# Five two-level products, added in DRAM, in the second stage of the two middle blocks

## The chip, the cores and the metric

The kernel runs on one core of one Trainium2 chip. The metric is the device time of an execution in microseconds; the figure for a kernel is the median of its runs. All arithmetic is fp32.

## What is computed

```python
def _L0_cond_ref(v, q, W3, b3, W2, b2):            # v: (64, 64, 512), q: (64, 256)
    q_emb = jax.nn.relu(q @ W3 + b3)
    n = v.shape[1]
    v_sum = jnp.sum(v, axis=1, keepdims=True)
    x = (n * v + v_sum) * q_emb[:, None, :]
    return jax.nn.relu(x @ W2 + b2)                # W2: (512, 512)

def _L0_ffn_ref(x, W_base, b_base, A_s, B_s, A_r, B_r, W_router, b_router):
    base_out = x @ W_base + b_base                 # W_base: (512, 512)
    shared_out = (x @ A_s) @ B_s                   # rank 16
    gates = softmax(x @ W_router + b_router)       # 6 experts, the best 2 count
    ...
    h = jnp.einsum('bsd,edr->bser', x, A_r)        # rank 16 each
    routed_out = jnp.einsum('bser,erf->bsf', h * w_per_e[..., None], B_r)
    return base_out + shared_out + routed_out

return x + _L0_ffn_ref(_L0_cond_ref(x, cond, ...), ...)
```

There are 4096 tokens of width 512, in 64 batches of 64. Each token goes through two products with a 512 x 512 matrix, a ReLU between them, and a low-rank term.

## The kernel before

**Blocks and stages.** The tokens are cut into NB = 4 blocks of 1024 (k = 0 to 3), each into two halves of TB = 512 columns; features lie on the partitions, in four chunks of 128. A block passes a first stage (`y = relu(x @ W2 + b2)`, in `first_mixed` for k = 0 and `first_inner` for the others) and a second stage (`out = x + y @ W_base + ...`, in `second`, and in `second_inner` for k = 3). Between them stand the low-rank matmuls with `a_sb` (`ph`, L1225), whose results `gate`, `weigh` and `turn` make into `hwT`, the weighted and transposed low-rank rows; `difference` makes `hwd`, the difference of its two halves.

**Seven products instead of eight.** Both 512 x 512 products are done by the Strassen-Winograd scheme: the operands are 2 x 2 in blocks of 256 features by 512 tokens, and seven products of block sums are combined. For the second stage the sums of `y` are made by `row_sums` (tile `sy`) and the sums of the weights are `tb`. With p1 to p7 the products, y = p1 + p6 and z = y + p7, the four output quarters are p1 + p2, y + p5 + p3, z + p4 and z + p5 (each with its share of the low-rank term and of x). The carried sums y and z are built by seeding: ScalarE copies one PSUM bank into another, and TensorE adds to it there. A plain product is done by `product`: for each of two output chunks, two matmuls of 512 columns (L181).

**Two levels.** A product can be done by the same scheme once more: seven matmuls of 128 x 128 x 256 (q(1) to q(7) in the code) instead of four of 512 columns. `inner_tools` has its steps. For product number t of its order, `open_banks(t)` takes two PSUM banks, `seed_y` and `seed_z` are ScalarE copies inside PSUM, and `take_w5`, `take_u`, `take_22`, `take_11`, `take_12` and `take_21` bring quarters out. A take without a summand (`plus` is None) is a ScalarE copy, except `take_22` and `take_12`, which add on VectorE to what lies in the destination. q(3) overwrites what `take_w5` reads, and q(4) what `take_22` reads. The sums of the moving operand (four operations of 128 x 256 each) are made by `inner_row_steps`, mostly on GpSimd. `row_places` says where they lie.

**Where which is used.** In the first stages of k = 1 to 3 all seven products are on two levels (matmuls at L488). In the second stage k = 0 has none, k = 3 has five (1, 2, 5, 4, 3), and k = 1 and 2 have two: products 1 and 2, in `two_products`, whose parts are handed to `second` through `two`. There products 3, 4, 5, 6 and 7 are plain. The routed term is a matmul of `bcat_sb` with `hwT` or `hwd` into the same banks (L778, 512 columns each), and the results are added to the rows of `x` (`res`, loaded by `load_rows`) by VectorE (`with_x`, `finish`, `leave`), from where SP's queue stores them.

**Order.** The order of instructions on each engine is written out by hand: an engine works through its list in the order of the calls, and waits at semaphores for the others. The next block's preparation is spread among the steps: `prepare(k + 1)` puts ScalarE's modulation of `x` (L224, 128 x 64 each, in pairs) on a list `behind`, from which `fill(n)` takes n pairs, and VectorE's sums for the next first stage on a list `held`, from which `sums_ahead(n)` takes n steps. GpSimd's part of the next first stage (`inner_two`, `s`, `inner_s`, `inner_late` at L334 to L337 and L278, then the sums at L585 and L588) comes in its list after all that the second stage gives it.

**Buffers.** `x` has three buffers (`xpool`), one of which becomes `wide`: the weight sums of products 5, 4 and 3, and the `parts` of two products. The tags `u`, `u22`, `u21` and `u12` hold the first stage's parts and then the rows of `x`. PSUM has six banks for products and two for `ph`, `pt`.

Of the kernel before, what the change touches and what calls it, by code (L numbers as in the profile page):

```python
# [10 lines left out]
F32 = mybir.dt.float32  # L11
# [27 lines left out]
def adaln_ffn(ctx: ExitStack, tc: tile.TileContext, xa, x0, x1, head, w3, w2, wb, a, bcat, bb, br, outT):  # L39
# [164 lines left out]
    def modulate(k):  # L204


        vs[k] = v = xs[k]
# [14 lines left out]
        def batch(c, b):  # L222
            x = v[:, c, :, ts(b, NH)]
            nc.scalar.activation(x, x, AF.Identity, bias=vsum[:, c, b : b + 1], scale=nq[:, c, b : b + 1])  # L224
# [71 lines left out]
    def prepare(k, also=()):  # L296
# [28 lines left out]
        behind.extend(pairs)  # L325
        if k == 1:
            behind.extend([step] for step in late + prepare_inner(k))
        else:

            held.extend(sums[c2] + sums[c3] + early + late[:3] + prepare_inner(k, late[3]))  # L330
# [9 lines left out]
    def prepare_inner(k, fourth=None):  # L340
# [37 lines left out]
        return first + steps("sums", of_s(all_of), nc.vector, all_of)  # L378
# [87 lines left out]
    def first_inner(k, y):  # L466
# [77 lines left out]
        open_banks(1)  # L544
        for t in range(2):
            q(1, t)
            q(5, t)
            seed_y(t)
            take_w5(t)
# [133 lines left out]
    def load_rows(k):  # L683

        res = {}
        for n, (f, h) in zip(pair_tags[2:3] + pair_tags[:2] + pair_tags[3:], ((1, 0), (1, 1), (0, 0), (0, 1))):
            res[f, h] = tmp.tile([P, KH, TB], F32, tag=n, name=f"x{n}_{k}")
            nc.sync.dma_start(
                res[f, h], x1[k, f * KH : (f + 1) * KH, :, ts(h, TB)].rearrange("c p t -> p c t")
            )  # L690
        return res

    def two_products(k, y, res):

        plain = mid.tile([P, 4, 4, R2], F32, tag="inner_s", name=f"inner_y_{k}")
        p1, p2 = wide["parts"][:, 0], wide["parts"][:, 1]
        operand = {1: y[:, :KH, 0], 2: y[:, KH:, 0]}
        s_side, sums_of = row_places(plain, lambda o: operand[o], {o: (o - 1, (0, 1, 2, 3)) for o in (1, 2)})
        tools = inner_tools(k, "h", (1, 2), low_side, s_side, {1: None, 2: None}, {1: p1, 2: p2})
        for o in (1, 2):  # L700
            for step in sums_of(o, lambda c, r, o=o: operand[o][:, c, ts(r, R2)], nc.gpsimd):
                step()

        def first_part():
            tools.open_banks(0)
            tools.q(1, 0)
            tools.q(5, 0)
            tools.seed_y(0)
            tools.take_w5(0)

        def second_part():
            tools.q(6, 0)
            tools.seed_z(0)
            tools.take_u(0)

        def third_part(ph):

            tools.open_banks(1)
            tools.q(1, 1)
            tools.q(5, 1)  # L720
            tools.seed_y(1)

            def first():
                tools.q(7, 0)
                tools.q(3, 0)
                tools.q(6, 1)
                tools.seed_z(1)
                tools.q(2, 0)
# [5 lines left out]
            tools.q(4, 0)  # L734
            tools.take_21(0)
            tools.q(7, 1)
            tools.take_22(1)
            tools.q(3, 1)
            tools.q(2, 1)

        def fourth_part(seeds):

            tools.take_u(1)
            tools.take_1(1)
            seeds[0]()
            tools.q(4, 1)
            seeds[1]()
            tools.take_21(1)
            tools.add(res[0, 0], res[0, 0], p2, nc.gpsimd)

        return {6: first_part, 7: second_part, "gate": third_part, "end": fourth_part, "p1": p1}

    def second(k, y, ph, res, two=None):
# [38 lines left out]
        ahead = [3, 0, 5, 1, 1, 2]  # L792

        def share():
            if two:
                sums_ahead(ahead.pop(0) if ahead else 0)
                return
# [5 lines left out]
        if two:  # L803
            copy_in = lambda name, j, source: nc.scalar.copy(bank(name, j), source)
            two["gate"](ph)
            weigh(k, ph)
            for j in range(KH):
                copy_in("y", j, two["p1"][:, j])
                prod(6, j, "y", start=False)
            fill(2)  # L810
            two["end"]([lambda j=j: seed("z", "y", j) for j in range(KH)])
            sums_ahead(2)
            for j in range(KH):
                u12[j] = with_x("y", j, KH + j, 0)
            for j in range(KH):
                copy_in("x", j, two["p1"][:, j])
            fill(2)
            prod(7, 0, "z", start=False)
            u22[0] = with_x("z", 0, KH, 1)
            sums_ahead(3)  # L820
            hwT = turn(k)
            prod(7, 1, "z", start=False)
            u22[1] = with_x("z", 1, KH + 1, 1)
            sums_ahead(1)
            fill(len(behind))
        else:
            gate(k, ph)
            prod(1, 0, "x")
            seed("y", "x", 0)
            prod(1, 1, "x")  # L830
            seed("y", "x", 1)
            prod(6, 0, "y", start=False)
            seed("z", "y", 0)
            prod(2, 0, "x", start=False)
            weigh(k, ph)
            u12[0] = with_x("y", 0, KH, 0)
            share()
# [451 lines left out]
```

## Time and profile before

| | |
|---|---|
| time, median of 3 runs | 257.36 us (257.3 to 257.56) |
| the profiled execution, its own time | 257.64 us |
| its span | 255.8 us |
| granted TensorE clock, mean | 0.998 |
| TensorE busy | 250.9 us in 1058 records |
| VectorE busy | 197.4 us in 389 |
| ScalarE busy | 152.2 us in 419 |
| GpSimd busy | 94.9 us in 116 |
| second stage, k = 1 (with the low-rank matmuls) | 94.6 to 133.4 us |
| first stage, k = 2 | 133.4 to 155.3 us |
| second stage, k = 2 | 155.3 to 194.1 us |
| stores, 256 KB each | 29, landing after 2.1 us |
| loads of rows of x, 512 KB each | 16, landing after 3.7 us |

The profile is of one execution; its span is the time from its first to its last instruction, and the execution's own time is longer by what lies around it. A fp32 matmul is two records in the trace. Records of TensorE are pipelined: the time from one start to the next is what a matmul costs, and it is shorter than the duration of a record. Line numbers (L488) are those of the kernel before. DMA transfers issued by SP are done by hardware queues; the trace of this kernel has no transfer issued by GpSimd.

### The profile page before, as it was taken

The page shows a single profiled execution, that of the slowest core. Times are in us where ns is not written, and L with a number is a line of the kernel's source. Part 1 is how long each engine was busy: PE and PEld are TensorE (multiplying, and loading weights), DVE is VectorE, ACT ScalarE, POOL GpSimd, SP SyncE. Part 2 cuts the span into 40 slices and gives each one's busy share as a digit, 9 for nine tenths or more (in the row PEclk, how much of TensorE's full clock was granted, in tenths as well). Part 3 has the DMA queues.
Part 4 walks back from the last instruction along what each step waited for, and adds up shares of the span by engine and source line. Part 5 has one row for each costly group of instructions (what it writes and reads, how often), then busy time and mean ns, then how long its engine had stood idle before and what let it go on. Part 6 is the DMA issues. An engine that isn't in the chain of part 4 may idle for free.

```text
span 255.8 us, 3426 instructions
## 1 busy us (share of the span) xinstructions
PE 250.9 (98%) x1058; PEld 175.8 (69%) x1058; DVE 197.4 (77%) x389; ACT 152.2 (59%) x419; POOL 94.9 (37%) x116
## 2 busy tenths in 40 slices
PE   8999999999999999999999999999999999999994
PEld 3755896454468889754458889955446889975783
DVE  2899998889967887895696797999296576887472
ACT  2299587688038799689306889689803427443220
POOL 1000000008008556037004988107200997039950
PEclk9999999999999999999999999999999999999999
DMA  6997729502420045000152023300044004400054
GB/s 179 383 342 271 309 67 379 210 3 83 163 82 0 3 129 195 6 3 0 46 201 83 0 86 110 138 3 0 0 164 164 0 0 157 175 3 1 0 184 143
DMA packets 14677, 28.55 MB, mean 112 GB/s; under 512 B 1490, under 2 KB 3538, under 8 KB 14659
## 3 DMA queue, kind: packets, MB, share of 16 engines
q1 hardware_dynamic: 14370, 28.08, 31.0%
q10 hardware_dynamic: 288, 0.26, 0.3%
q8 instruction: 8, 0.13, 0.2%
q14 instruction: 11, 0.08, 0.1%
HBM read 19.94 MB, written 8.39 MB: 111 GB/s over the span
## 4 chain that ended last, share of the span: by engine, by line
PE 94%; ACT 2%; DMA 2%; SPq 0%; issue 0%; DVE 0%
PE ia L488 13%; PE ph L1225 11%; PE ib L488 10%; PE oz L181 9%; PE ow L181 8%; PE py L395 5%; PE oy L181 5%; PE ja L894 4%; PE ow L778 4%; PE jb L894 4%; PE ha L894 3%; PE ox L181 3%; PE hb L894 2%; PE oz L778 2%; PE ox L778 2%; DMA w_sb<-in_w_dram 2%
## 5 line engine op out<-in xcount | busy, mean ns | idle before, releaser
L224 ACT ACTIVATE x<-x,vsum,nq 128x64 f32<-128x64 f32 x192 | 67.6, 433 | 1.3 <-DVE vsum L220 1.3
L1225 PEld LDWEIGHTS ph<-a_sb,y 128*128 128x128 f32 x256 | 30.9, 192 | 1.6 <-ACT y L381 0.7
L1225 PE MATMUL ph<-a_sb,y 128*128 128x118 f32 x256 | 31.4, 276 | 0.3 <-ACT y L381 0.3
L494 ACT COPY ib<-ia 128x256 f32<-128x256 f32 x21 | 7.5, 359 | 39.5 <-PE ia L488 39.5
L479 DVE TENSOR_TENSOR u<-ib,u 128x256 f32<-128x256 f32 x42 | 16.4, 417 | 14.0 <-PE ib L488 14.0
L639 POOL TENSOR_TENSOR hwd<-hwT 113x512 f32<-113x512 f32 x4 | 5.5, 1363 | 57.2 <-ACT hwT L634 57.2
L334 POOL TENSOR_TENSOR inner_two<-x 128x256 f32<-128x256 f32 x3 | 2.2, 725 | 48.7 <-PE ib L488 48.7
L479 DVE TENSOR_TENSOR u<-ia,u 128x256 f32<-128x256 f32 (+1 forms) x36 | 16.1, 461 | 5.0 <-ACT u L526 2.9
L381 ACT ACTIVATE y<-u,head_sb 128x256 f32<-128x256 f32 (+1 forms) x30 | 15.8, 584 | 3.6 <-DVE u L454 3.0
L488 PE MATMUL ib<-inner_s,inner_t 128*128 128x256 f32 x60 | 17.8, 384 | 0.0
L218 DVE TENSOR_REDUCE vsum<-x 128x8 f32<-128x512 f32 x24 | 15.4, 674 | 0.0
L181 PE MATMUL oz<-sy,tb 128*128 128x512 f32 x32 | 15.0, 593 | 0.0
L395 PE MATMUL py<-v,w_sb 128*128 128x512 f32 (+1 forms) x40 | 14.4, 510 | 0.3 <-DMA w_sb<-in_w_dram 0.3
L181 PE MATMUL oy<-sy,tb 128*128 128x512 f32 x32 | 14.6, 594 | 0.0
L887 POOL TENSOR_TENSOR xu<-xu,inner_tb 128x1024 f32<-128x1024 f32 x2 | 4.7, 2362 | 24.0 <-ACT inner_tb L910 24.0
L497 ACT COPY ib<-ib 128x256 f32<-128x256 f32 x21 | 7.6, 363 | 9.0 <-PE ib L488 8.9
L488 PEld LDWEIGHTS ib<-inner_s,inner_t 128*128 128x128 f32 x60 | 11.2, 190 | 2.2 <-ACT ib L497 0.8
L262 ACT ACTIVATE v<-x,vsum,nq 128x64 f32<-128x64 f32 x32 | 11.0, 428 | 1.9 <-DVE vsum L260 1.9
L275 DVE TENSOR_TENSOR s<-x 128x512 f32<-128x512 f32 x6 | 4.9, 824 | 9.3 <-ACT x L224 9.2
L395 PEld LDWEIGHTS py<-v,w_sb 128*128 128x128 f32 x40 | 7.4, 190 | 6.3 <-issue 4.5
L181 PE MATMUL oz<-y,tb 128*128 128x512 f32 x24 | 11.3, 592 | 0.0
L181 PE MATMUL ow<-sy,tb 128*128 128x512 f32 x24 | 11.3, 592 | 0.0
(270 smaller groups left out, 609.2 us busy)
## 6 DMA issues: line engine op xcount, KB each, us to landing
xu<-in_x_dram SPq DMA_DIRECT2D x16, 512.0 KB, 3.7
out_dram<-xu SPq DMA_DIRECT2D x29, 256.0 KB, 2.1
x<-in_x_dram SPq DMA_DIRECT2D x12, 512.0 KB, 7.6
x<-in_x_dram SPq DMA_DIRECT2D x7, 256.0 KB, 5.6
w_sb<-in_w_dram SPq DMA_DIRECT2D x4, 256.0 KB, 5.6
wb_sb<-in_wb_dram SPq DMA_DIRECT2D x4, 256.0 KB, 5.3
out_dram<-xu SPq DMA_DIRECT2D x4, 128.0 KB, 1.7
w_sb<-in_w_dram SPq DMA_DIRECT2D x1, 384.0 KB, 5.2
```

The lines of the kernel that those rows point to most:

```text
L181: nc.tensor.matmul(ps, w[i][:, c, ts(j, P)], s[i][:, c, :], start=start and c == 0, stop=c == KH - 1, skip_group_check=True,)
L218: nc.vector.tensor_reduce(vsum[:, c, bs], xc, AX.XY, ALU.add)
L224: nc.scalar.activation(x, x, AF.Identity, bias=vsum[:, c, b : b + 1], scale=nq[:, c, b : b + 1])
L262: nc.scalar.activation(v[:, c, :, ts(b, NH)], batches_of(c, b, b + 1)[:, :, 0], AF.Identity, bias=vsum[:, c, b : b + 1], scale=nq[:, c, b ...
L381: nc.scalar.activation(y[:, f, h, cols], src, AF.Relu, bias=b2_sb[:, f : f + 1])
L395: nc.tensor.matmul(p[:, :, lo * NH : hi * NH], w2_sb[:, c, ts(f, P)], v[:, c, :, lo * NH : hi * NH], start=(c == 0 and lo == 0), stop=(c = ...
L479: add = lambda o, a, b: nc.vector.tensor_tensor(o, a, b, ALU.add)
L488: nc.tensor.matmul(bank[b, t][:, cols], t_side(o, n), s_side(o, n), start=n == 1, stop=True, skip_group_check=True,)
L497: nc.scalar.copy(bank["b", t][:, hi], bank["b", t][:, lo])
L778: nc.tensor.matmul(ps[name, j], bcat_sb[:, ts(f, P)], hw, start=False, stop=True, skip_group_check=True)
L894: nc.tensor.matmul(p, w, s, start=start, stop=True, skip_group_check=True)
L1225: nc.tensor.matmul(ph[:, h * NS + s, :HC], y[:, c, h, ts(s, P)], a_sb[:, c, :], start=(c == 0), stop=(c == NC - 1),)
```

## The change

In blocks k = 1 and 2 the second stage is done by a new function, `second_between`, in place of `two_products` and of the branches of `second` for it. Products 1, 2, 4, 5 and 3 are on two levels, in this order; 6 and 7 stay plain. Each of the five leaves PSUM without a summand, into its own place (`parts`: two in `wide`, three in quarters of `y` that are no longer read), and GpSimd's queue then adds it onto the output in DRAM (`to_rows`, `accum_op=ALU.add`), product 5 onto two quarters. The quarter (0, 0) of the output is first filled with the rows of `x` by a copy from DRAM to DRAM on SP's queue (`load_rows`); the other three are stored by `with_x` with the sums that hold products 6 and 7, and products 3, 4 and 5 are added onto these. The routed term is added to the two-level products by matmuls of 256 columns (`with_routed`).

With it: the fourth sum of `sy` goes from VectorE to GpSimd; eight of the modulations of the last chunk go from ScalarE to VectorE (k > 1, `modulate`), and `prepare` orders them accordingly; the weight sums of `wide` are made from block 0 on, and GpSimd's steps for them stand before and after the first stage of k = 1; and `load_x(3)` moves from block 0 to block 1, behind `load_rows`.

```diff
         def batch(c, b):
             x = v[:, c, :, ts(b, NH)]
-            nc.scalar.activation(x, x, AF.Identity, bias=vsum[:, c, b : b + 1], scale=nq[:, c, b : b + 1])
+            scale, bias = nq[:, c, b : b + 1], vsum[:, c, b : b + 1]
+            if k > 1 and c == CHUNKS[-1] and b >= BB // 2:
+                nc.vector.tensor_scalar(x, x, scale, bias, ALU.mult, ALU.add)
+            else:
+                nc.scalar.activation(x, x, AF.Identity, bias=bias, scale=scale)
...
-            held.extend(sums[c2] + sums[c3] + early + late[:3] + prepare_inner(k, late[3]))
+            n = len(pairs) - BB // 4
+            behind.extend(pairs[:n])
+            first, inner_sums = prepare_inner(k, late[3])
+            held.extend(sums[c2] + sums[c3] + early + first + sum(pairs[n:], []) + late[:3] + inner_sums)
...
+            if (f, h) == (0, 0) and 0 < k < NB - 1:
+                nc.sync.dma_start(outT[k, :KH, h], x1[k, :KH, :, ts(h, TB)])
+                continue
...
+    def second_between(k, y, res):
+        order = (1, 2, 4, 5, 3)
...
+        sy_steps = sy_steps(fourth=nc.gpsimd)
...
+        parts = {1: wide["parts"][:, 0], 2: wide["parts"][:, 1], 4: y[:, :KH, 1], 5: y[:, :KH, 0], 3: y[:, KH:, 0]}
+        tools = inner_tools(k, "h", order, wide["t"], s_side, dict.fromkeys(order), parts)
...
+        routed_of = {2: ("first", 0), 4: ("second", 0), 5: ("second", KH), 3: ("less", KH)}
...
+        def to_rows(o, f, h):
+            nc.gpsimd.dma_start(
+                outT[k, f : f + KH, h].rearrange("f p t -> p f t"), parts[o], accum_op=ALU.add
+            )
+
+        def with_x(x, name, j, f, h):
+            add(x[:, j], bank[name, j], x[:, j])
+            nc.sync.dma_start(outT[k, f + j, h], x[:, j])
...
+        def start(t):
+            open_banks(t)
+            q(1, t)
+            q(5, t)
+            tools.seed_y(t)
+            tools.take_w5(t)
+
+        def sixth(t):
+            q(6, t)
+            tools.seed_z(t)
+            tools.take_u(t)
+
+        def seventh(t):
+            q(7, t)
+            routed(t, 22)
+            tools.take_22(t)
+
+        def second_and_third(t):
+            q(3, t)
+            q(2, t)
+
+        def ends(t):
+            routed(t, 1)
+            tools.take_1(t)
+            q(4, t)
+            routed(t, 4)
+            tools.take_21(t)
+
+        for o in (1, 2, 4):
+            inner_sums(o)
+
+        def main_part(ph):
...
+            gate(k, ph, (first, lambda: tools.take_12(0)))
+            q(4, 0)
+            tools.take_21(0)
+            second_and_third(1)
+            to_rows(1, 0, 0)
+            weigh(k, ph)
+            for j in range(KH):
+                seed(j, "y", parts[1][:, j])
+                product(bank["y", j], 6, j, tb, sy, start=False)
+            fill(2)
+            tools.take_u(1)
+            sums_ahead(2)
+            for j in range(KH):
+                seed(j, "z", bank["y", j])
+                with_x(x12, "y", j, KH, 0)
+            run(sy_steps[3:])
+            inner_sums(5)
+            fill(2)
+            product(bank["z", 0], 7, 0, tb, sy, start=False)
+            with_x(x22, "z", 0, KH, 1)
+            with_x(x21, "z", 0, 0, 1)
+            sums_ahead(2)
+            hwT = turn(k)
...
+            product(bank["z", 1], 7, 1, tb, sy, start=False)
+            with_x(x22, "z", 1, KH, 1)
+            seventh(1)
+            with_x(x21, "z", 1, 0, 1)
+            hws["less"] = difference(k, hwT)[:GB]
+            inner_sums(3)
+            start(2)
+            fill(2)
+            q(4, 1)
+            routed(1, 4)
+            tools.take_21(1)
+            routed(1, 1)
+            tools.take_1(1)
+            to_rows(2, 0, 0)
+            sums_ahead(2)
+            sixth(2)
+            fill(2)
+            start(3)
+            seventh(2)
+            sums_ahead(5)
+            second_and_third(2)
+            sixth(3)
+            fill(2)
+            ends(2)
+            to_rows(4, 0, 1)
+            sums_ahead(8)
+            start(4)
+            seventh(3)
+            sums_ahead(3)
+            second_and_third(3)
+            sixth(4)
+            ends(3)
+            to_rows(5, KH, 1)
+            to_rows(5, KH, 0)
+            sums_ahead(2)
+            seventh(4)
+            sums_ahead(2)
+            second_and_third(4)
+            ends(4)
+            to_rows(3, KH, 0)
...
         if k == 0:
             first_mixed(y)
+            wide_sums()
         else:
+            if k == 1:
+                for step in wide["steps"][0]:
+                    step()
             rest = first_inner(k, y)
+            if k == 1:
+                for step in wide["steps"][1]:
+                    step()
+        res = load_rows(k)
         if k == 1:
-            wide_sums()
-        res = load_rows(k)
-        if k == 0:
             load_x(3)
...
-        two = second_inner(k, y, res) if k == NB - 1 else two_products(k, y, res) if k else None
+        two = second_inner(k, y, res) if k == NB - 1 else second_between(k, y, res) if k else None
```

## The prediction

> **What bounds the kernel now.** I read the page's busy shares and its chain of waits first, then the windows by stage, then the timelines of the second of the four blocks (k=1) and of the stage behind it. Page:
>
> ```profile
> span 255.8 us, 3426 instructions
> PE 250.9 (98%) x1058; PEld 175.8 (69%) x1058; DVE 197.4 (77%) x389; ACT 152.2 (59%) x419; POOL 94.9 (37%) x116
> ...
> PE 94%; ACT 2%; DMA 2%; SPq 0%; issue 0%; DVE 0%
> ```
>
> The chain of waits runs 94% over TensorE. The windows show the two changed second stages (first and third row) and the first stage between them:
>
> ```profile
> core 0: us, PE busy (x) PEld busy (x) DVE busy (x) ACT busy (x) POOL busy (x), PEclk, DMA share, GB/s
> 94.61:133.36 38.75, 38.75 (x155) 24.09 (x156) 30.78 (x54) 25.41 (x70) 13.17 (x13) 1.00 0.22 75
> 133.36:155.30 21.94, 21.78 (x100) 18.17 (x99) 17.59 (x40) 17.00 (x50) 15.56 (x19) 1.00 0.18 61
> 155.30:194.05 38.75, 38.75 (x155) 24.08 (x156) 30.95 (x54) 25.42 (x70) 12.14 (x13) 1.00 0.21 75
> ```
>
> TensorE has no idle time there and clock 1.00, so fewer matmul columns shorten the block if the engines that feed it keep up. The chain in order of time prices the columns:
>
> ```profile
> 117.89 1.72 PE ow L181 x4
> ...
> 137.53 1.29 PE ia L488 x6
> 138.83 0.86 PE ib L488 x4
> ```
>
> A 512-column record costs 1.72/4 = 0.43 us, a 256-column one 0.86/4 = 0.215; one fp32 matmul is two records.
>
> **The change part by part.** The profiled run's own time is 257.64 us (span 255.8 and 1.8 around it), 0.28 above the median 257.36. What follows are differences within the execution, added to the median.
>
> *TensorE.* Products 3, 4 and 5 lose 3 x 8 records of 512 and gain 3 x 14 of 256: 42 x 0.215 - 24 x 0.43 = -1.29 us a block. The routed term is 16 records of 512 before, 32 of 256 after: nothing. Weight loads stay hidden (190 ns by the page's LDWEIGHTS rows, under a pitch of 215).
>
> *A wait uncovered.* q(7,1) moves from ahead of q(3,1) to behind product 7. In the timelines:
>
> ```profile
> 106.11 0.65 ACT L910 COPY inner_tb<-ha 128x256 f32<-128x256 f32 x2
> ...
> 106.34 0.60 PE L894 MATMUL hb<-inner_y,low_t 128*128 128x256 f32 x2
> 106.90 0.67 PE L894 MATMUL ha<-inner_y,wb_sb 128*128 128x256 f32 x2
> ```
>
> 106.34 is q(7,1), 106.90 is q(3,1), which overwrites what ScalarE's second copy (to 106.76) reads. It cannot start sooner, so product 6 starts about 0.13 earlier, not 0.43: TensorE's gain is -0.97.
>
> *VectorE* loses the fourth sum (1.21) and six 512-column adds (6 x 0.68), gains six 256-column adds (6 x 0.42) and eight tensor_scalars of 128x64 (0.185 undisturbed for that shape at L217, 1.5 in all): -1.3. Less work, but later deadlines: q(4,t) overwrites the bank half that take_22(t) reads. Adding the rows from product 6 at 107.7, q(4,4) is due near 131.7. On VectorE three sums (0.65 each), take_12(3) and two 0.87 sums stand ahead of take_22(4), which ends near 132.0: +0.3. Ahead of take_22(1) stand two sums with both inputs in SBUF, beside GpSimd's hwd. The row of 147.64 below (1.20 for an operation that elsewhere takes 0.17, beside a 1.25 us GpSimd operation) says that such a meeting costs up to 1 us; here, after slack, 0 to 0.85, taken as 0.3. So TensorE alone: about -0.35 a block, between -0.97 and +0.2.
>
> *ScalarE* gains 18 evacuations at 0.36, loses two 0.52 copies and eight modulations at 0.36: +2.6 on 25.4. Walking the order, seed_y(3) comes about 0.2 late for q(6,3); the range has it. If its modulations fell later still, each 1.43 us group would show in full at the next seed.
>
> *SP and early parts.* load_x(3) moves from block 0 to behind load_rows of block 1: four issues near 0.4 each. x_3 is first summed after 133 and loads took 7.6 us to land, so nothing. GpSimd's moved weight sums (about 6 us) lie in its idle stretches at 63 to 77 and 91 to 93.6: nothing; without that cover 2 us at the next sums. The x rows of quarter (0,0) are now copied DRAM to DRAM, ahead of x21's load on SP.
>
> *That copy* is weighed against the skill. The row below gives 3.7 us for 512 KB. The Trainium skill, "DMA: Bandwidth & Descriptors", section "Why a DMA increments its semaphore by 16 and not by 1", says that the slowest dimension sets how many engines share a transfer; here it is 2, so two engines. By the trace's packets (31.0% of 16 x 255.8 us over 14370 = 88 ns, about 2 KB each) that is 128 x 88 ns = 11.3 us: from 93.9 to about 107. By the row nothing waits. By the rule to_rows(1), ready at 107.1, is just met, and so is x21, queued behind it and needed at 113.7: nothing either. I take the rule, and keep a copy at half that rate for a rival.
>
> *GpSimd* gains three quartets of sums (12 x 0.73), the fourth sum (2.36) and six transfers; it loses one add (2.36) and four weight sums. Sums for product 5 are ready near 114 to 116 and due at 119.8; product 3's near 120, due 124.7: hidden. The transfers at the block's end are not. to_rows(3) adds onto rows that to_rows(5) has just added onto, so GpSimd waits there for a landing, and behind it in its queue stand the next block's sums:
>
> ```profile
> 137.61 0.72 POOL L334 TENSOR_TENSOR inner_two<-x 128x256 f32<-128x256 f32 x1 [16.73 <-PE ib L488]
> ...
> 150.11 2.50 POOL L588 TENSOR_TENSOR u<-u,u 128x512 f32<-128x512 f32 x2
> ...
> 147.64 1.20 DVE L220 TENSOR_TENSOR vsum<-vsum,q_sb 128x16 f32<-128x16 f32 x1
> ...
> 152.64 0.42 DVE L479 TENSOR_TENSOR u<-ia,u 128x256 f32<-128x256 f32 x1 [0.17 <-POOL u L588]
> ...
> 153.68 0.59 PE L488 MATMUL ia<-inner_late,t 128*128 128x256 f32 x2
> ```
>
> From 137.61 GpSimd works without a pause to 152.61; VectorE waits for it at 152.64 and TensorE needs that add (to 153.06) at 153.68. GpSimd may start 0.6 us late and no more; beyond that TensorE stands still one for one. Product 6's other consumer there, e3, has about 1 us.
>
> When is it free? The two to_rows(5) follow take_12(3), near 130.1 by the walk. The trace has no GpSimd transfer and no accumulating one. The nearest rows:
>
> ```profile
> DMA packets 14677, 28.55 MB, mean 112 GB/s; under 512 B 1490, under 2 KB 3538, under 8 KB 14659
> ...
> q1 hardware_dynamic: 14370, 28.08, 31.0%
> ...
> xu<-in_x_dram SPq DMA_DIRECT2D x16, 512.0 KB, 3.7
> out_dram<-xu SPq DMA_DIRECT2D x29, 256.0 KB, 2.1
> ```
>
> 16 packets an engine at 88 ns are 1.4 us for 512 KB, so a 256 KB store's 2.1 us are 0.7 moving and 1.4 of receipt. An accumulating transfer must also read its destination: between 1.4 and, with twice the reading, 2.8 us; I take 2.4. Issuing takes SP 0.34 to 0.39 us; [...]between 0.4 and 2, I take 1.2 (an estimate, three times SP's). Then: 130.1 + 1.2 issue + 2 x 2.4 moving + 1.4 receipt + 1.2 to issue to_rows(3) = 138.7, which is 1.1 later than 137.61, less 0.6 of slack: +0.5 a block, and TensorE's gain is lost in that wait. The same skill page, section "Anatomy of one DMA", fits 2.0 us + bytes/436 GB/s to a plain transfer of GpSimd's: 3.2 us for 512 KB, and calls descriptor generation small. With 0.4 for issuing, the second ends at 130.1 + 0.8 + 3.2 plus at most 1.2 of queueing, and GpSimd is free at 135.7: no stall, and TensorE's -0.35 stands. That rule speaks for the change; it says nothing of the second read, so I lean to the packet sum.
>
> The sum: +0.55 a block, twice: 257.36 + 1.1 = **258.5 us**. The last block has its matmuls unchanged.
>
> **The rivals.**
> (1) *The wait for the landing decides (forecast).* Place: GpSimd before inner_two. With issue d and moving m it decides from d + m above about 3.1 us; at d = 1.5 and m = 3.5 it is +2 x 3.3 = 264. For it: GpSimd's unbroken 15 us. Against: no row for either size.
> (2) *Landing in time, TensorE's columns decide.* d + m under 2.8. -0.35 a block, up to -0.97, gives 256.7 down to 255.4; about 256.4. For it: 98% TensorE, and a store that lands in 2.1. Against: the walk's late take_22.
> (3) *The two cancel*, within 0.5 us of 257.36, d + m near 3.
> (4) *The copy on two engines is slow*: above 150 ns a packet it ends after 113, x21 comes later still, and VectorE stands before the add of x21 with take_22(1) behind it. At 176 ns: 22.5 us, to 117; x21 at 118, 4 us late in each block: 265.
> That the change doesn't do what it says is ruled out by the changed instruction order: fourteen 256-column records for each of the five products.
>
> **How the numbers follow.** 0.2% is 0.5 us, about what a measurement of this kernel can tell from no change. (1) 0.42, (2) 0.36, (3) 0.14, (4) 0.08: faster 0.36, same 0.14, slower 0.50. Range 255.4 (all of -0.97 twice) to 263.0 (d + m near 4.7), leaving out half of (4) and the ends of (1). The likeliest case's own range is 257.9 to 262.
>
> **What would show it.** In the profile after: GpSimd's wait for a transfer before L343 inner_two at k=2 and 3, its start against the first L498 matmul (4.4 us before), transfers of about 1.2 us issue and 4 to 6 us to landing; an LDWEIGHTS or matmul wait for VectorE at L498 near the first stage's end; 256-column records at 0.215. Wrong if inner_two still waits for TensorE (then rival 2), if the copy lands beyond 113 (rival 4), or if TensorE idles inside the second stage by more than 1 us a block.

## The result and the profile after

| | before | after |
|---|---|---|
| time, median | 257.46 us (257.3 to 257.85, 4 runs) | 271.31 us (269.76 to 272.72, 4 runs) |
| ratio | | 1.0534, 95% interval 1.0465 to 1.0603 |
| profiled execution: time, span | 257.64, 255.8 us | 272.72, 270.9 us |

The change costs 13.9 us. 258.5 us was forecast, with a range up to 263.0: the sign was right, the size was not. The profiled execution after is the slowest of the four, so the account below splits 15.1 us, 1.2 more than the medians differ by. The head of the page after, with the shares of the chain of waits:

```profile
span 270.9 us, 3658 instructions
PE 254.9 (94%) x1126; PEld 190.8 (70%) x1126; DVE 201.7 (74%) x403; ACT 157.5 (58%) x435; POOL 131.4 (48%) x152
...
PE 57%; DVE 19%; POOL 10%; ACT 7%; issue 4%; DMA 1%; SPq 0%; DVEq 0%; POOLq 0%; ACTq 0%
```

TensorE held 94% of the chain before and holds 57% now; VectorE and GpSimd have 29%. The waits of TensorE, in total, times and longest, say where (there were none of these before):

```profile
PE hb L979 <- DVE inner_tb L972: 4.4, 2, 2.4
PE ia L498 <- DVE inner_late L489: 3.6, 2, 2.1
PE ia L498 <- DVE u L489: 1.1, 1, 1.1
PE hb L979 <- DVE y L972: 0.9, 2, 0.4
PE ha L979 <- ACT inner_tb L995: 0.8, 2, 0.4
```

L979 is a two-level product of the second stage, L498 one of the first stage behind it. Cutting the profiled executions at the first matmul of product 6 (the first of tile `oy`), the first at L498 and the first of the next `ph` gives the account that the rest of this text uses. Before, the middle second stage ran from 107.84 to 133.20, now from 107.78 to 137.05, and so on (us):

| stretch | before | after | |
|---|---|---|---|
| second stage, k = 1, from product 6 | 25.36 | 29.27 | +3.9 |
| first stage, k = 2 | 21.34 | 25.18 | +3.8 |
| second stage, k = 2, from product 6 | 25.36 | 29.62 | +4.3 |
| first stage, k = 3 | 21.00 | 24.42 | +3.4 |
| all else | 162.7 | 162.4 | -0.3 |

So there are two losses of nearly the same size, one inside the second stage and one behind it, and each comes twice.

**The loss in the second stage.** VectorE's timeline after, at k = 1, then GpSimd's, then TensorE's (start, duration, engine, line, operation, tiles, and in brackets the idle time before it with its releaser):

```profile
111.19 2.08 DVE L221 TENSOR_TENSOR vsum<-vsum,q_sb 128x16 f32<-128x16 f32 x1
...
115.58 1.18 DVE L280 TENSOR_TENSOR s<-x 128x512 f32<-128x512 f32 x1
116.80 1.64 DVE L281 TENSOR_TENSOR s<-s,x 128x512 f32<-128x512 f32 x1
118.36 0.68 DVE L972 TENSOR_TENSOR xu<-oz,xu 128x512 f32<-128x512 f32 x1
118.96 0.41 DVE L972 TENSOR_TENSOR inner_tb<-hb,inner_tb 128x256 f32<-128x256 f32 x1
```

```profile
109.51 1.33 POOL L738 DMA_DIRECT2D out_dram<-inner_tb  x1 [4.43 <-DVE w L692]
110.41 2.81 POOL L283 TENSOR_TENSOR sy<-y,sy 128x1024 f32<-128x1024 f32 x1
...
116.18 1.71 POOL L650 TENSOR_TENSOR hwd<-hwT 113x512 f32<-113x512 f32 x1
```

```profile
119.42 0.70 PE L979 MATMUL hb<-y,low_t 128*128 128x256 f32 x2 [2.00 <-DVE inner_tb L972]
119.96 0.61 PE L979 MATMUL hb<-hwT,bcat_d 113*128 113x256 f32 x2
120.39 1.88 PE L979 MATMUL ha<-hwT,bcat_sb 113*128 113x256 f32 x4
122.07 1.06 PE L979 MATMUL hb<-inner_y,inner_tb 128*128 128x256 f32 x2
```

The 16-column product at L221 takes 0.17 to 0.18 us when nothing meets it. Here it takes 2.08, and it ends with GpSimd's fourth sum (110.41 to 113.22), which the change has put there. The two sums at L280 and L281 take 0.68 and 0.69 undisturbed and 1.18 and 1.64 here, beside the inner sums and `hwd`. take_22(1), the last row of VectorE, stands behind all three, and q(4,1) at 119.42 waits 2.00 us for it (2.36 at k = 2, where the operation held up most by the fourth sum is `w` at L692, 2.72 instead of 0.21). The Trainium skill, "SBUF — State Buffer", section "Who interferes with whom", fits these rows: a VectorE operation with two inputs in SBUF contends with a GpSimd operation that reads SBUF.

Then the clock. Windows of the same execution (us, busy time and count by engine, granted clock, DMA share, GB/s):

```profile
core 0: us, PE busy (x) PEld busy (x) DVE busy (x) ACT busy (x) POOL busy (x), PEclk, DMA share, GB/s
117.00:120.41 3.41, 1.41 (x7) 0.90 (x7) 2.97 (x4) 1.97 (x6) 3.33 (x4) 1.00 0.45 168
120.41:123.82 3.41, 3.41 (x10) 2.66 (x9) 1.10 (x3) 1.37 (x4) 1.16 (x3) 0.50 0.27 100
124.00:126.00 2.00, 2.00 (x11) 1.74 (x10) 0.97 (x3) 1.82 (x6) 0.66 (x1) 1.00 0.51 59
```

After the idle 2 us TensorE is granted half its clock. The eight records from 120.39 to 123.78 start 0.42 us apart instead of 0.215: 1.7 us more. 2.0 of waiting and 1.7 of half clock are the 3.7 that this stage loses beside its smaller items.

**The loss behind it.** GpSimd's timeline after, from the last transfers of k = 1 into the first stage of k = 2:

```profile
134.37 2.44 POOL L738 DMA_DIRECT2D out_dram<-y  x2 [3.17 <-DVE y L972]
144.41 1.20 POOL L738 DMA_DIRECT2D out_dram<-y  x1 [7.59 <-ACT x L229]
145.16 1.21 POOL L343 TENSOR_TENSOR inner_two<-x 128x256 f32<-128x256 f32 x1
...
158.17 2.49 POOL L599 TENSOR_TENSOR u<-u,u 128x512 f32<-128x512 f32 x2
```

and what comes of it on VectorE and TensorE:

```profile
156.90 0.42 DVE L489 TENSOR_TENSOR inner_late<-ia,inner_late 128x256 f32<-128x256 f32 x1 [3.89 <-POOL inner_late L596]
...
157.38 0.70 PE L498 MATMUL ia<-inner_s,w_sb 128*128 128x256 f32 x2 [2.14 <-DVE inner_late L489]
```

This is the mechanism of the forecast. The two to_rows(5) are issued by 136.81, and to_rows(3), which adds onto the same rows, only 7.59 us later. GpSimd's unbroken 15 us start that much later (the releaser named, an activation, is merely the event that came last; the plain writes below show that it is the transfer). TensorE stands 2.14 us, and again gets half clock: 0.93 in the mean over this stage's 25.18 us is 1.8 us. At k = 3 it stands 1.51 and 1.07 us, without a loss of clock; the rest of the 3.4 us there is in the records around these waits, which start 0.3 to 0.4 us apart instead of 0.215. What the transfers are made of:

```profile
q1 hardware_dynamic: 13766, 27.03, 28.5%
q0 software_dynamic: 3264, 6.29, 16.2%
...
out_dram<-y POOLq DMA_DIRECT2D x8, 512.0 KB, 5.9
```

q0 is GpSimd's queue: 16.2% of 16 engines for 270.9 us over 3264 packets is 215 ns a packet, against 90 on the hardware queue (28.5% over 13766). A transfer is 272 packets, 17 an engine: 3.7 us of moving, and 5.9 from issue to landing.

### The profile page after: what moved, and what is told of

Its sections match the earlier page's. It is cut to its first block, busy times and chain, and to the rows that moved or that the text cites. A ratio compares the mean times of both kernels' runs of the same rounds, so it can differ in the third digit from the quotient of the medians.

```text
span 270.9 us, 3658 instructions
## 1 busy us (share of the span) xinstructions
PE 254.9 (94%) x1126; PEld 190.8 (70%) x1126; DVE 201.7 (74%) x403; ACT 157.5 (58%) x435; POOL 131.4 (48%) x152
## 3 DMA queue, kind: packets, MB, share of 16 engines
q1 hardware_dynamic: 13766, 27.03, 28.5%
q0 software_dynamic: 3264, 6.29, 16.2%
## 4 chain that ended last, share of the span: by engine, by line
PE 57%; DVE 19%; POOL 10%; ACT 7%; issue 4%; DMA 1%; SPq 0%; DVEq 0%; POOLq 0%; ACTq 0%
PE ph L1317 11%; PE ia L498 6%; PE py L405 5%; PE ha L979 5%; PE ib L498 5%; ACT x L229 4%; PE hb L979 4%; PE ja L979 4%; PE jb L979 3%; PE oy L181 3%; PE ox L181 3%; PE oz L181 3%; DVE xu L972 2%; DVE s L281 2%; DVE s L280 1%
## 5 line engine op out<-in xcount | busy, mean ns | idle before, releaser
L229 ACT ACTIVATE x<-x,vsum,nq 128x64 f32<-128x64 f32 x176 | 62.9, 432 | 1.6 <-DVE vsum L221 1.6
L738 POOL DMA_DIRECT2D out_dram<-y x8 | 9.7, 1330 | 31.6 <-ACT y L995 10.8
L498 PE MATMUL ib<-inner_s,inner_t 128*128 128x256 f32 x60 | 17.9, 386 | 0.1
L498 PEld LDWEIGHTS ib<-inner_s,inner_t 128*128 128x128 f32 x60 | 11.1, 190 | 2.7 <-ACT ib L507 0.8
L738 POOL DMA_DIRECT2D out_dram<-inner_tb x4 | 4.9, 1236 | 13.7 <-DVE inner_tb L972 5.9
L181 PEld LDWEIGHTS oy<-sy,tb 128*128 128x128 f32 x32 | 5.9, 190 | 6.6 <-issue 6.2
L498 PE MATMUL ia<-s,t 128*128 128x256 f32 x36 | 10.2, 379 | 0.0
L181 PEld LDWEIGHTS oz<-sy,tb 128*128 128x128 f32 x32 | 5.8, 190 | 5.8 <-issue 5.7
```

What stands on the lines that cost most here:

```text
L181: nc.tensor.matmul(ps, w[i][:, c, ts(j, P)], s[i][:, c, :], start=start and c == 0, stop=c == KH - 1, skip_group_check=True,)
L229: nc.scalar.activation(x, x, AF.Identity, bias=bias, scale=scale)
L498: nc.tensor.matmul(bank[b, t][:, cols], t_side(o, n), s_side(o, n), start=n == 1, stop=True, skip_group_check=True,)
L738: nc.gpsimd.dma_start(outT[k, f : f + KH, h].rearrange("f p t -> p f t"), parts[o], accum_op=ALU.add)
```

## The experiments

Each edit is made to the changed kernel unless its text says otherwise. "Before" on the same chips was 257.5 to 257.8 us.

**The copy over 16 engines.** The copy from DRAM to DRAM is issued at 93.91 and to_rows(1), which adds onto it, at 109.51, 2.5 us after product 1 was ready.

```diff
-                nc.sync.dma_start(outT[k, :KH, h], x1[k, :KH, :, ts(h, TB)])
+                nc.sync.dma_start(
+                    outT[k, :KH, h].rearrange("f p t -> p f t"),
+                    x1[k, :KH, :, ts(h, TB)].rearrange("f p t -> p f t"),
+                )
```

> Edit: the copy of the rows of x from DRAM to DRAM is written with the 128 partitions as its outer dimension on both sides. Two-engine theory (the copy's first dimension of 2 puts it on two DMA engines, so it lands 15 us after its issue and holds GpSimd's first transfer back from 107 to 109.5): the transfer is issued near 107.1. If the late copy is the cause of TensorE's 2.0 us idle before q(4,1), that idle and the half clock behind it go in both blocks: about -7 us, 264. If the cause is GpSimd's fourth sum against VectorE, whenever it comes, the sum only meets the gate's operations 2 us sooner in place of the vsum product: 0 to -2 us, 269.5 to 271.5.

Measured: 274.77 us (272.95 to 275.92), ratio 1.0664 (1.0619 to 1.0709): 3.5 slower than the change, which none of the expectations had. The copy now lands in 5.3 us and to_rows(1) goes out at 107.51, two us sooner. But with it GpSimd's fourth sum comes two us sooner, into the gate. VectorE's timeline of this run:

```profile
107.63 3.92 DVE L688 TENSOR_TENSOR gt<-gt,eq 128x288 f32<-128x288 f32 x1
```

L688 takes 0.46 us in the change. Here it overlaps GpSimd's issue of to_rows(1) and the fourth sum (108.41 to 111.22), and ends 0.3 us behind the sum. The issue alone does not do this: at k = 2 of the run with the fourth sum on VectorE (below) L688 starts 0.2 us into such an issue and takes 0.46. Taking the copy's lateness away does not take the loss away: the late copy had kept the fourth sum clear of most of the gate.

**Product 5 added to product 3 on GpSimd.** The second to_rows(5) is left out; its part reaches DRAM with product 3's.

```diff
             to_rows(5, KH, 1)
-            to_rows(5, KH, 0)
...
+            add(parts[3], parts[3], parts[5], nc.gpsimd)
             to_rows(3, KH, 0)
```

> Edit: product 5 is added to product 3 in SBUF by GpSimd (128 x 1024, about 2.4 us) and leaves with it, so the second transfer of product 5 is gone, and no transfer adds onto rows that another has just added onto. Landing theory (GpSimd stands 7.6 us for a landing before to_rows(3), and the next first stage's sums behind it are 3.8 us late): inner_two waits for TensorE again, the idle at the end of the first stages of k=2 and 3 and the half clock behind it go: about -7 us, 264. Rival (GpSimd simply has too much to do, the landing only fills time it would need anyway): less than -2 us, above 269.

Measured: 264.97 us (262.54 to 265.9), ratio 1.0275 (1.0224 to 1.0326), 6.3 faster than the change. inner_two starts at 139.79 instead of 145.16, TensorE's waits at L498 are down to 0.6 us in all, and the two first stages take 21.60 and 21.56 us. The wait for the landing is worth 6 of the 13.9 us. The wait before q(4,1) stays, with 1.34 us at k = 1 (no half clock behind it) and 2.36 at k = 2 (half clock): the second stages take 27.19 and 30.27 us.

**The fourth sum back on VectorE.**

```diff
-        sy_steps = sy_steps(fourth=nc.gpsimd)
+        sy_steps = sy_steps()
...
-            run(sy_steps[3:])
...
-            "sums": lambda: run(sy_steps[:3]), ...
+            "sums": lambda: run(sy_steps), ...
```

> Edit: the fourth sum of sy goes back to VectorE, before the gate, as in the kernel before. Fourth-sum theory (a small VectorE product stands 1.9 us behind the 2.8 us sum on GpSimd, and take_22(1) and q(4,1) behind it): idle before q(4,1) falls from 2.0 to under 1 us, too short for the half clock: -5 to -6 us in all, about 265.5. Rival (the s sums on VectorE meeting hwd and the inner sums do it, the fourth sum being hidden): -2 us at most, 269 or more, with the idle still there.

Measured: 267.67 us (266.85 to 269.14), ratio 1.0401 (1.036 to 1.0442), 3.6 faster than the change, less than the 5 to 6 expected. At k = 1 VectorE's timeline shows both meetings gone, though only one was touched: the sums now come before `hwd`, and it is `hwd` that is held up (1.72 us instead of 1.27 in the run of the late sums below):

```profile
111.99 0.18 DVE L221 TENSOR_TENSOR vsum<-vsum,q_sb 128x16 f32<-128x16 f32 x1
...
114.77 0.68 DVE L280 TENSOR_TENSOR s<-x 128x512 f32<-128x512 f32 x1
115.49 0.69 DVE L281 TENSOR_TENSOR s<-s,x 128x512 f32<-128x512 f32 x1
```

At k = 2 L281 still takes 1.78 us. q(4,1) does not wait at k = 1 and waits 0.55 at k = 2. The second stages take 25.83 and 26.47 us, and the first stages stay at 24.74 and 24.44.

**The idle time filled.** q(1) and q(5) of the third product are done three times: 1.72 us of matmuls more a block, just ahead of q(4,1).

```diff
         def start(t):
             open_banks(t)
-            q(1, t)
-            q(5, t)
+            for _ in range(3 if t == 2 else 1):
+                q(1, t)
+                q(5, t)
```

> Edit: q(1) and q(5) of the third product in the order (t = 2) are done three times instead of once, in the place where TensorE would stand before q(4,1): 8 records, 1.7 us more of work in each of the two blocks, the same results. Clock theory (the doubled pitch of 0.43 us for 256-column records behind the idle is the granted clock at one half, and idle of about 2 us brings it): idle is below 0.5 us, the clock stays at 1.00 there, and the time falls by about 1.7 us a block: 268, although work is added. Rival (the pitch is stretched by something else, such as the transfers under way or the waits of single matmuls): unchanged or longer, 271 to 274.

Measured: 269.52 us (269.23 to 270.54), ratio 1.048 (1.0456 to 1.0503): 1.8 faster than the change with 3.4 us of work added. Only half of the gain that was expected. In its profile q(4,1) comes at 119.49, as in the change, since VectorE sets it; but the granted clock is 1.00 throughout, the records behind it are 0.215 apart, and the second stages are 27.55 and 28.21 us long, 1.7 and 1.4 shorter. The clock after the wait is a cost of its own. It is not paid to the same amount in every execution, which would explain why the median gains less than the profile: estimated as span times (1 - mean clock), the four executions of the change lost 5.4, 2.4, 0.5 and 1.6 us to the clock, 2.5 in the mean, and those of this run 0.4.

**Plain writes.** This one leaves out a part of the computation, as its expectation says.

```diff
-                outT[k, f : f + KH, h].rearrange("f p t -> p f t"), parts[o], accum_op=ALU.add
+                outT[k, f : f + KH, h].rearrange("f p t -> p f t"), parts[o]
```

> The five transfers out of each middle block write without accum_op; the additions onto the output rows are left out. Sizes what the addition itself costs the transfer. If the 215 ns a packet of the software queue are the addition's, packets come to near the 90 ns of the hardware queue, a transfer lands 2 us sooner (3.7 instead of 5.8), to_rows(3) is issued some 3 to 4 us sooner than at 144.4, TensorE's idle time at the first L498 falls from 2 us to under 0.5 and the kernel gains 4 to 6 us (265 to 267). If the cost is that of the software queue whatever it carries, packets and landing stay within 0.5 us and the time within 1 us of the changed kernel.

Measured: 264.24 us (263.95 to 264.39), ratio 1.0241 (1.0203 to 1.0279), 7.1 faster. The queues and the transfers of this run:

```profile
q0 software_dynamic: 1728, 6.29, 6.4%
...
out_dram<-y POOLq DMA_DIRECT2D x8, 512.0 KB, 3.2
```

and GpSimd:

```profile
132.65 1.45 POOL L738 DMA_DIRECT2D out_dram<-y  x2 [3.65 <-DVE y L972]
137.93 0.72 POOL L738 DMA_DIRECT2D out_dram<-y  x1 [3.84 <-DVE vsum L221]
139.74 0.72 POOL L343 TENSOR_TENSOR inner_two<-x 128x256 f32<-128x256 f32 x1 [1.08 <-PE ib L498]
```

The same 6.29 MB in half the packets, 155 ns each: the queue's engines are busy 269 us instead of 702 for them. A transfer lands in 3.2 us, is issued in 0.72 instead of 1.2, and to_rows(3) follows 3.84 us after the others instead of 7.59. inner_two waits for TensorE again, as before the change, and the first stages take 21.01 us both times. It is the addition in DRAM that is dear, not GpSimd's queue as such.

**The s sums later.** VectorE's two sums at L280 and L281 are put behind take_22(1).

```diff
             with_x(x21, "z", 0, 0, 1)
-            sums_ahead(2)
             hwT = turn(k)
...
             with_x(x21, "z", 1, 0, 1)
+            sums_ahead(2)
             hws["less"] = difference(k, hwT)[:GB]
```

> The two s sums of VectorE are put behind the last with_x(x21) instead of before turn, so that take_22(1) no longer stands behind them; nothing else changes. If the s sums' meeting with hwd and the inner sums (the forecast's term) made the 2.0 us before q(4,1), the wait falls under 0.5 us, the granted clock stays at 1.00 there and the kernel gains 5 to 6 us. If GpSimd's fourth sum made most of it, by holding vsum's product 2 us, the wait stays at 1 us or above, though short enough to leave the clock alone, and the kernel gains 2 to 4 us.

Measured: 265.72 us (265.06 to 266.41), ratio 1.0303 (1.0252 to 1.0355), 5.6 faster. The second stages take 25.83 and 26.01 us and the wait before q(4,1) is 0.2 in all, although the fourth sum still holds L221 for 1.47 us at k = 1 and L692 for 2.65 at k = 2. Number and wait are those of the first theory, but the edit does more than undo a meeting: it also takes the s sums' own 1.37 us from ahead of take_22(1). How the meetings add can be read from the profiled stages that have the change's order there (us; the hold-up is the time of L692, L221, L280 and L281 beyond 0.21, 0.17, 0.68 and 0.69):

| stage | VectorE held up | q(4,1) waits | difference |
|---|---|---|---|
| the change, k = 1 | 3.36 | 2.00 | 1.36 |
| the change, k = 2 | 3.72 | 2.36 | 1.36 |
| plain writes, k = 1 | 2.52 | 1.16 | 1.36 |
| plain writes, k = 2 | 3.71 | 2.36 | 1.35 |
| product 5 on GpSimd, k = 1 | 2.70 | 1.34 | 1.36 |

So 1.36 us is VectorE's slack there. (At k = 2 of the last run 4.10 us go with a wait of 2.36, but TensorE is already 0.3 us late at `pt`.) In the run of the late s sums the slack is 1.36 + 1.37, and the 1.30 and 2.86 us of hold-up that are left give no wait at k = 1 and 0.18 at k = 2, as they should. So neither theory is the whole. The fourth sum is the larger part, 1.9 of the change's 3.36 us at k = 1 and 2.5 of the 3.72 at k = 2. Alone it would leave waits of 0.5 and 1.2 us, and the other meetings alone 0.1 and none: estimates from the slack, not runs.

**Both repairs.** Product 5 on GpSimd and the fourth sum on VectorE.

> The fourth sum back on VectorE and product 5 added to product 3 in SBUF by GpSimd, together. If the two waits (before q(4,1), and for inner_two) are the whole loss and independent, their single gains of 3.6 and 6.3 us add to 261.5; with the clock never falling the sum reaches further, to 258 to 260. If they hide one another (one wait's removal only uncovers the other), it stays at 263 to 265. TensorE's waits at L498 under 1 us in all, those before q(4,1) under 1 us in all, granted clock 1.00.

Measured: 261.4 us (261.03 to 263.66), ratio 1.015 (1.0094 to 1.0207): the sum of the two gains (6.3 and 3.6, giving 261.4). With executions of one kernel up to 3 us apart, the match to the digit is luck, but the two losses add, as independent ones do. TensorE waits 0.6 us at L498 and 1.1 before q(4,1), in all, and the second stages take 26.38 us. The profiled execution is the slowest of the four, 263.66: at 5.0 us TensorE stood 2.11 us for a load of weights, and the half clock followed there, not in the middle blocks.

**Both repairs and two moves on VectorE.** The s sums as above, and

```diff
-            sums_ahead(2)
             seventh(4)
-            sums_ahead(2)
+            sums_ahead(4)
             second_and_third(4)
```

> The kernel before this one with two moves on VectorE: the s sums behind the last with_x(x21), and seventh(4) ahead of the first two sums of inner_s, against the 0.5 us before q(4,1) and the 0.43 us before q(4,4). If these waits are all that is left, TensorE has no wait over 0.3 us in the two middle second stages and gains 1.5 to 2 us on the kernel before this one; the forecast's sum without GpSimd's lateness (fewer columns, one uncovered wait of 0.4 us) would then put it at 256 to 258. If ops merely trade places on VectorE, it stays within 0.5 us of the kernel before this one.

Measured: 260.7 us (260.55 to 261.18), ratio 1.0108 (1.007 to 1.0147), 0.7 faster and short of the 1.5 to 2 expected. The second stages are at 25.13 and 25.21, for the first time below the 25.36 of before; but TensorE, now earlier, meets GpSimd at L498 (2.2 us in all): the first stages rise from 21.60 and 21.58 to 22.50 and 22.46. GpSimd had spent 2.35 us on adding product 5 and issued to_rows(3) at 137.78.

**That addition on VectorE.** The kernel just above, with product 5 added to product 3 by VectorE.

```diff
-            add(parts[3], parts[3], parts[5], nc.gpsimd)
+            add(parts[3], parts[3], parts[5])
```

> As the kernel of both repairs and the two moves (260.7 us), with the sum of products 5 and 3 on VectorE instead of GpSimd, which takes 2.35 us there. If what is left is GpSimd's chain of sums starting late (inner_two at 138.6 instead of 137.6), inner_two starts a microsecond sooner, the 1.1 us waits at L498 vanish, the first stages come to 21.0 to 21.5 us as before the change, and the kernel gains 1.5 to 2.5 us: 258.2 to 259.2, within half a per cent of the kernel before. If VectorE's own work at the start of the first stage is the limit, its 1.2 us more puts u and inner_late off and the time stays at 260 to 261.

Measured: 259.1 us (259.03 to 259.25), ratio 1.0062 (1.0049 to 1.0075). The waits of TensorE in the stages at issue, and two stages by window:

```profile
PE ha L977 <- ACT inner_tb L993: 0.6, 2, 0.3
PE hb L977 <- ACT y L993: 0.5, 2, 0.2
PE ib L498 <- DVE u L489: 0.3, 1, 0.3
...
107.98:133.11 25.13, 24.89 (x104) 18.57 (x104) 20.87 (x43) 15.54 (x45) 12.72 (x13) 1.00 0.68 144
133.11:155.09 21.98, 21.53 (x97) 17.90 (x96) 17.62 (x40) 17.70 (x53) 16.15 (x19) 1.00 0.39 71
```

The time is within what was expected, as is the first stage of k = 3 (21.33); that of k = 2 is half a microsecond above. With the two losses and the waits behind them taken away, at clock 1.00 in these stages, 12.2 of the 13.9 us are gone. It is still 0.6% slower than before.

**The modulations back on ScalarE.** The kernel just above with the change's eight tensor_scalars turned back into activations. Their place is not turned back: they stay on the list `held`, where the change put them for VectorE, and do not return to `behind`, from which `fill(2)` gave them to ScalarE four at a time.

```diff
-            if k > 1 and c == CHUNKS[-1] and b >= BB // 2:
-                nc.vector.tensor_scalar(x, x, scale, bias, ALU.mult, ALU.add)
-            else:
-                nc.scalar.activation(x, x, AF.Identity, bias=bias, scale=scale)
+            nc.scalar.activation(x, x, AF.Identity, bias=bias, scale=scale)
```

> The kernel before this one with the last chunk's modulation back on ScalarE alone (the eight tensor_scalars of the change undone). If they cost VectorE something that counts (the forecast took 1.5 us of work that lies beside other work, so nothing), the kernel gains up to 1 us; if ScalarE's activations of x gate the first stage's use of x instead, it loses 0.5 to 2 us; otherwise within 0.3 us of the kernel before this one.

Measured: 262.59 us (262.4 to 264.56), ratio 1.0207 (1.0183 to 1.0231): 3.5 slower than the kernel above, more than any of its expectations. ScalarE's timeline, and TensorE's:

```profile
126.11 2.76 ACT L226 ACTIVATE x<-x,vsum,nq 128x64 f32<-128x64 f32 x8
128.77 0.37 ACT L982 COPY hb<-ha 128x256 f32<-128x256 f32 x1
```

```profile
129.28 0.67 PE L974 MATMUL hb<-sy,inner_tb 128*128 128x256 f32 x2 [1.46 <-ACT hb L982]
```

Eight activations in a row stand ahead of a seed, and TensorE waits 1.46 us in each block. At this place in the order ScalarE has no room for them. What they would cost ScalarE spread out on `behind`, as before the change, was not run.

## Why the forecast missed

Two steps failed, each for about half of the loss, and a term was missing in both stages, the clock's. VectorE's hold-up before q(4,1) was booked at 0.3 us, and the waits there are 2.00 and 2.36. The moving time of an adding transfer was taken as 2.4 us and is 3.7; the first stages lose 3.8 and 3.4 us instead of the 0.5 that it left.

*TensorE's columns: right.* 42 records of 256 columns at 0.215 for 24 of 512 at 0.43 hold in the timelines. From product 6 on the forecast's -1.29 is -0.86, since q(7,1) moved in (0.43). The kernel without the losses has -0.23: most of the difference is the wait for ScalarE's evacuation before q(7,2), where two records start 0.62 us apart instead of 0.215. The uncovered wait at q(3,1) was forecast, and is there (0.40 a block in the change), as is q(4,4)'s for take_22(4): 0.3 forecast, 0.43 measured.

*"0 to 0.85, taken as 0.3": the step that failed first.* It saw VectorE's sums meet `hwd`. It booked the fourth sum as 1.21 us less for VectorE and 2.36 more for GpSimd, and did not ask what VectorE would be doing beside it. The two meetings hold VectorE up by 1.9 (L221) and 1.5 us (L280 and L281); TensorE waits 2.0 and 2.36. The runs of the fourth sum and of the late s sums show that either move ends nearly all of the wait, and the slack of 1.36 us how the two add. The meeting that the forecast counted would alone have left 0.1 us at most, so its 0.3 was near enough for that; the one that it did not look for is the larger part. The forecast's closing condition, more than 1 us of idle time inside the second stage, is what happened.

*No term for the clock.* Every wait was priced one for one. The waits of 2.0 to 2.4 us cost another 1.7 us each, three times in the profiled execution and less often in the others; the filled idle time shows that this part is the clock's.

*"I take 2.4": the mis-sized term.* GpSimd's landing wait was the forecast's own mechanism, and its issue of 1.2 us was right to the digit. Moving took 3.7 us, not 2.4, outside the bounds of 1.4 to 2.8. The forecast had 16 packets an engine at 88 ns, doubled for the upper bound; there are 17, of about the same size, and each takes 215 ns, 2.4 times as long. By the forecast's own sum, with 3.7 for 2.4 twice, GpSimd is 2.6 us later: 3.1 us a block instead of 0.5, so 263.7 in all, just above the range; its price at 3.5 with 1.5 of issue was 264. Put to the times at which the last two transfers were really issued (134.37 and 202.56), the sum with 3.7 has to_rows(3) at 144.4 and 212.6; it was issued at 144.41 and 211.94. The first stages lost 3.8 and 3.4, the first with 1.8 of half clock in it. Two slips of the sum change nothing: 0.5 a block was entered as 0.55, and its own terms put the threshold of d + m at 3.4, not 3.1.

*The skill's plain price.* The forecast weighed the 2.0 us + bytes/436 GB/s of "DMA: Bandwidth & Descriptors", section "Anatomy of one DMA" (an estimate of 3.2 us for 512 KB), and set it aside because it says nothing of the second read. The plain writes landed in 3.2 us, as that rule has it, and the adding ones in 5.8 to 5.9.

*The copy: right in kind, not in size.* It ran on two engines, as the skill's rule has it and not the row's 3.7 us: from 97.60 to 99.50 the DMA share after is 0.13, two of 16. to_rows(1) went out 15.6 us after it, 2.5 late, where the forecast had 11.3 us of moving and an end at about 107, just in time. Rival (4) falls: no add of x21 waits for its rows in the profile after, and the run that sped the copy up lost 3.5 us.

*ScalarE and the tensor_scalars: no sign against them.* No wait of TensorE for ScalarE in the middle blocks is longer than 0.4 us in the profile after. The warning that modulations falling late would show in full at the next seed (1.43 us) is what the last run shows (1.46).

Rival (2) was the change's best case, 256.4. With its waits taken away the kernel stands at 259.1. What is left open is the last 1.6 us: of the profile's 1.0 us of longer span, 0.64 and 0.33 lie in the two first stages, 0.3 from product 6 of the last block on and 0.1 ahead of the middle blocks, and the second stages give 0.46 back; another 0.4 lies outside the span (2.2 us between span and time, 1.7 to 1.8 before). They were not tried one by one. No version run beats the kernel before.

## What to carry to other kernels

Work moved to an idle GpSimd had two prices here: its own time, and that of the VectorE operations with two inputs in SBUF that met it, with all that is queued behind those. So look up what stands on VectorE in that window, and add the meetings up against one slack. A transfer that adds in DRAM should be priced apart from a store, by its packets, and the last one of a chain should not stand ahead of work that the next stage waits for. And a wait of TensorE of about 2 us or more may be paid for twice.

## What was unexpected of the hardware

The granted clock fell to 0.50 after short waits. In the profiled executions of the change and of the experiments eight waits of 2.00 to 2.36 us were each followed by 3.4 us at 0.50; the thirteen between 1.34 and 1.98 us were not followed by any fall. The Trainium skill, "TensorE: Matmul & The Clock Gate", section "HAM oscillation — how this bites in real kernels", warns of gaps above about 3.4 us; here 2.0 was enough. The place of the wait counts as well. Within a profile the falls start whole multiples of 3.413 us apart (120.41, 157.96 and 188.68 in the change are 11 and 9 steps apart, 120.31 and 188.58 in the run of the copy 20), and each lasts one step. Counted in these steps, TensorE was idle for 2.00 to 2.36 us of the step ahead of each of the eight falls (117.00 to 120.41 in the windows above is one), and up to 1.80 us in a step brought none. The wait of 1.98 us, in the run of the copy, lay across the end of a step at 226.12, with 1.48 us ahead of it. So the same wait may bring a fall in one execution and none in another; that would explain, though it was not traced, why the four executions of the changed kernel had mean clocks of 0.980, 0.991, 0.994 and 0.998 (272.72, 270.38, 272.23 and 269.76 us).

A VectorE operation of 0.46 us took 3.92 beside GpSimd's fourth sum (L688 in the run of the copy). A transfer with addition took 215 ns a packet of about 1.9 KB, a plain one of the same queue 155 ns for 3.6 KB, and the hardware queue's packets, loads and stores together, 90 ns for about 2 KB.
